# The first gated group's keys and values computed as blocks of Strassen's method beside the last cross-attention section

## The chip, the cores and the metric

The kernel runs on one core of one Trainium2 chip. The metric is the device time of one execution in microseconds (us). Five engines work side by side, each through its own queue in program order: PE (TensorE, matrix products), DVE (VectorE), ACT (ScalarE), POOL (GpSimd) and SP (SyncE, which here issues the transfers). They wait for each other through semaphores.

## The reference

Sixteen sequences of 128 tokens with 512 features, all in float32, pass through one decoder layer and one gated cross-attention layer:

```python
# decoder layer (16 heads of 32)
qkv = layernorm(x) @ w_qkv + b_qkv
x = x + attention(q, k, v, ltor_mask) @ w_ao + b_ao
q = layernorm(x) @ w_q + b_q;  k, v = split(ctx @ w_kv + b_kv)
x = x + attention(q, k, v, cross_mask) @ w_co + b_co
x = x + gelu(layernorm(x) @ w1 + b1) @ w2 + b2            # 512 -> 2048 -> 512
# gated layer
a = layernorm(ctx)
Q = x @ Wq.T;  K = a @ Wk.T;  V = a @ Wv.T
x = x + tanh(gate) * (attention(Q, K, V, key_mask) @ Wo.T)
```

## The kernel before

**Groups and sections.** The sixteen sequences are four groups of four (`NG`, `GB`). A section is one kind of attention for one group: A0 to A3 (self), B0 to B3 (cross), and, after the MLP, D0 to D3 (gated). `attend` runs the sections through one software pipeline. A section has 16 steps, 0 to 15, four for each sequence ("batch"); a unit is four heads of a batch, one per step. In `step` number k the following is put on the queues, in this order: at each fourth step the product of probabilities and values of an earlier batch (`av`, in `mix`) and the scores of a new one (`sc`, in `scores`); transfers that fetch turned probabilities (`receive_pair`); what was deferred by `afterwards` and is now run by `due()`; the jobs planned for this step; an output projection (`mo`); then the softmax of several units at once: `turn_unit` for unit k-3 (a DVE transpose and a transfer to DRAM, `away`), `norm_unit` for unit k-2 (a DVE reciprocal `sum`, then a POOL multiplication `s<-s,sum`), `least_unit` and `exp_unit` for unit k-1 (a DVE minimum `mn`, then four ACT exponentials), and `scale_unit` and `add_mask` for unit k (a DVE multiplication `s<-sc,mask`, then a POOL addition `s<-s,mask`). In the last batch of B3 the mask is instead added on DVE in four custom instructions with the minimum (`mask_and_least`), and POOL has no addition there.

**Jobs.** `jobs` of the next section, or `beside_last_cross` for B3, return a plan: which job is put on the queues in which step. The order on the queues is therefore written by hand, in lists of steps. `prepare` of a later object runs beside, one call per step: in B2's steps it is that of `FirstGated`, which normalizes the context of the first gated group (tile `T_a0`, four chunks scaled on ACT at steps 12 to 15) and fetches the turned weights `w_gk` and `w_gv`.

**Projections.** There are two ways to multiply weights with 512 tokens. `project_chunk` and `values_chunk` make one chunk of 128 outputs with four matmuls of 512 columns, and ACT copies the chunk out. `block_product` makes the same as seven products of half-size blocks (Strassen's method): four matmuls of 256 columns each, on sums of blocks that `left_blocks` and `right_blocks` describe as four additions on each side. Products 1, 6 and 7 collect in one PSUM bank and are copied out by ACT; products 5, 2, 4 and 3 are added by DVE to what stands there. The cross section's own keys and values are made in this way.

**Beside B3.** `gated_start` makes keys and values of the first gated group from `T_a0` (names `k_D0`, `v_D0`) by `project_chunk` and `values_chunk`, a chunk at each of steps 1, 2, 3, 5 and 7, 9, 13, 15, and keeps them in DRAM for later. `mlp_start` normalizes group 0 for the MLP (`ml_send`: DVE statistics, a POOL power `rstd_C`, a DVE `off_C`, an ACT scaling `ln_C`, a DVE transpose and a transfer) and gets it back turned (`back_C`, four ACT scalings to `T_C` at steps 12, 13, 14, 14). `piece` advances the generator `mlp`, which loads the first MLP weights, makes four sums of `w1_0` on POOL (`t<-w`), four sums of `T_C` on POOL (`sx`; `token_sums`), and from step 17 on the MLP's products `h`, in the order `H_ORDER`. The second of these reads the third `sx` sum. The MLP follows without a break.

Of the kernel before, what the change touches and what calls it, by code (L numbers as in the profile page):

```python
# [16 lines left out]
P = 128  # L17
# [37 lines left out]
def decoder_then_gated_cross_attention(ctx: ExitStack, tc: tile.TileContext, a: dict, out: bass.AP):  # L55
# [24 lines left out]
    def afterwards(engine, do):  # L80
        late[engine].append(do)
# [185 lines left out]
    def act_tile(name, tag="actT"):  # L267
        return work.tile([P, KC, TG], F32, tag=tag, name=f"T_{name}", bufs=2 if tag == "enc" else 1)
# [69 lines left out]
    def project_chunk(t, wt, actT, c, name, bias=None, bias0=0, bank="mm"):  # L338

        mm = ps(bank, f"mm_{name}_{c}")  # L340
        for k in range(KC):
            nc.tensor.matmul(mm, wt[:, k, c * P : (c + 1) * P], actT[:, k, :], start=(k == 0), stop=(k == KC - 1))
        if bias is None:
            afterwards("act", lambda: nc.scalar.copy(t[:, c], mm))
        else:
            afterwards("act", lambda: nc.scalar.activation(t[:, c, :], mm, AF.Identity, bias=col(bias, bias0 + c)))

    def values_chunk(v, wt, actT, b, name):

        mm = ps("mm", f"mm_{name}_{b}")  # L350
        for k in range(KC):
            nc.tensor.matmul(mm, actT[:, k, b * S : (b + 1) * S], wt[:, k, :], start=(k == 0), stop=(k == KC - 1))
        afterwards("act", lambda: nc.scalar.copy(v[:, b, :], mm))
# [17 lines left out]
    def left_blocks(wt, t):  # L371


        (a11, a21), (a12, a22) = halves(wt)
        s3, s2, s4, s1 = (*t, a21)[:4]
        return [a11, a12, s4, a22, s1, s2, s3], [
            (s3, a11, a21, ALU.subtract), (s1, a21, a22, ALU.add), (s2, s1, a11, ALU.subtract),
            (s4, a12, s2, ALU.subtract),
        ]
# [110 lines left out]
    def by_quarters(t):  # L490
# [18 lines left out]
        {10: (1,), 11: (2,), 12: (6,), 13: (5, 7), 15: (4, 3)},  # L509
    )  # L510
    FIRST_CROSS_BLOCKS = {6: (1,), 7: (2, 6), 8: (5,), 9: (7, 4), 11: (3,)}, CROSS_BLOCKS[1]
    GATED_BLOCKS = (
# [492 lines left out]
    class CrossAttention(Section):  # L1005
# [59 lines left out]

        v_bias = "b_cv", 0

        def tokens_again(self, at_, order=range(3)):
            return [([lambda b=b: fetch_part(f"x_{self.name}", x[self.g], b) for b in order], at_)]

# [74 lines left out]
    def mlp_start(ml):  # L1145

        ml.b2 = load_row(a["L0_xattn_b2"], "b2_row")
        ml.db1 = cpool.tile([P, NF], F32, tag="db1", name="db1")
        for i in range(NI):
            b1, c0 = columns["b1"]  # L1150
            c0 += i * KC
            nc.vector.tensor_tensor(
                ml.db1[:, 2 * i : 2 * i + 2], b1[:, c0 + 2 : c0 + 4], b1[:, c0 : c0 + 2], ALU.subtract
            )

        def row_difference():
            ml.db2 = work.tile([P, H], F32, tag="row", name="db2_row", bufs=2)
            nc.vector.tensor_tensor(ml.db2[:, 0:HF], ml.b2[:, HF:H], ml.b2[:, 0:HF], ALU.subtract)

        ml.lnT = []  # L1160
        def start():
            ml.lnT.append(act_tile("C0"))
            ml_begin(0)

        sends = [lambda b=b: ml_send(0, b) for b in range(GB)]
        back = [lambda k=k: chunk_back(ml.lnT[0][:, k], ml.back, k, "ln3_s", "ln3_b") for k in range(KC)]
        return (
            ([start, row_difference, lambda: ml_receive(0)], [0, 5, 7]), (sends, [0, 1, 2, 3]), (back, [12, 13, 14, 14]),
            ([lambda m=m: ml.part(m) for m in range(NQ)], [7, 7, 9, 9])
        )  # L1170

    def ml_begin(g):
# [2 lines left out]
    def ml_receive(g):  # L1175
        ml.back, ml.part = receiver(f"C{g}", ml.away)
# [4 lines left out]
    def mlp(ml, last_steps):  # L1181
# [8 lines left out]
        def sums_of(g, t):  # L1190
            s3, s2, s4 = (quarter(work, "s", f"sx{n}_{g}", 7) for n in range(3))
            quarters = [[t[i][:, :, j * HF : (j + 1) * HF] for j in range(2)] for i in range(2)]
            return token_sums(quarters, s3, s2, s4)
# [5 lines left out]
        def load(n, which):  # L1199
            g, i = steps[n]  # L1200
            ap, r0, c0 = (a["L0_xattn_w1"], 0, i * H) if which == 1 else (a["L0_xattn_w2"], i * H, 0)
            wt = wpool.tile([P, KC, H], F32, tag="w", name=f"w{which}_{n}")
            src = ap[r0 : r0 + H, c0 : c0 + H].rearrange("(k p) n -> p k n", p=P)
            if n < 2 and not (n == 1 and which == 2):
                for k in range(KC):
                    pieces.append(lambda k=k: nc.sync.dma_start(out=wt[:, k], in_=src[:, k]))
            elif g == 0:
                nc.sync.dma_start(out=wt, in_=src)
            else:
                nc.sync.dma_start(out=wt[:, 0:2, 0:HF], in_=src[:, 0:2, 0:HF])  # L1210
                nc.sync.dma_start(out=wt[:, 2:4, :], in_=src[:, 2:4, :])
            return wt
# [114 lines left out]

        w1[0] = load(0, 1)
        yield
        w2[0], w1[1] = load(0, 2), load(1, 1)  # L1330
        right1[0], todo, _ = sums(0, 1, "enc", w1.pop(0), nc.gpsimd)
        yield
        for do in todo:
            do()
            yield
        sides, todo = sums_of(0, [ml.lnT[0][:, 0:2], ml.lnT[0][:, 2:4]])
        for do in todo:
            do()
# [67 lines left out]
    def keep_part(key, t, n):  # L1406

        if n == 0:
            gated[key] = dram.tile(list(t.shape), F32, tag=f"kept_{key}", name=f"kept_{key}")
        nc.sync.dma_start(out=gated[key][:, n], in_=t[:, n])  # L1410
# [50 lines left out]
    class FirstGated:  # L1461


        def prepare(self, p):
            if p == 0:
                self.raw = work.tile([P, GB, H], F32, tag="enc", name="enc_D0", bufs=2)
                self.ln, self.away = ln_tile("D0"), away_tile("D0")
            if p in (0, 1):
                for b in (2 * p, 2 * p + 1):
                    nc.sync.dma_start(out=self.raw[:, b, :], in_=a["ctx_2048"][b])  # L1470
            elif p >= 2 * GB:
                key, k = ("gk", "gv")[p // GB - 2], p % GB
                if k == 0:
                    w[key] = wpool.tile([P, KC, H], F32, tag="w", name=f"w_{key}")
                nc.sync.dma_start(out=w[key][:, k], in_=gated[key][:, k])
            if 2 <= p < 6:
                q = p - 2
                normalize_and_send(self.raw[:, q, :], self.ln[:, q], self.away, "D0", q)
            if p >= 12:
                if p == 12:  # L1480
                    next(in_mlp)
                ml.pieces.popleft()()
            if p in (9, 11):
                if p == 9:
                    self.back, self.part = receiver("a0", self.away)
                for m in range(2):
                    self.part(m + 2 * (p == 11))
            if p >= 12:
                if p == 12:
                    self.aT = act_tile("a0", "enc")  # L1490
                group_back(self.aT, self.back, "gamma", "beta", [p - 12])

    def gated_start(first):

        first_k = work.tile([P, KC, TG], F32, tag="kT", name="k_D0", bufs=2)
        first_v = work.tile([P, GB, H], F32, tag="v", name="v_D0", bufs=2)

        def key_job(c):
            project_chunk(first_k, w["gk"], first.aT, c, "k_D0")
            afterwards("act", lambda: keep_later("k_D0", first_k, c, c != 1))  # L1500

        def value_job(b):
            values_chunk(first_v, w["gv"], first.aT, b, "v_D0")
            afterwards("act", lambda: keep_later("v_D0", first_v, b, True))

        def keep_later(key, t, n, wait):
            if wait:
                afterwards("act", lambda: keep_part(key, t, n))
            else:
                keep_part(key, t, n)  # L1510

        return (
            ([lambda c=c: key_job(c) for c in range(KC)], [1, 2, 3, 5]),
            ([lambda b=b: value_job(b) for b in range(GB)], [7, 9, 13, 15]),
        )

    class GatedAttention(Section):
# [206 lines left out]
    def beside_last_cross():  # L1724
        flip[0], in_blocks[0] = 2, False
        def piece():
            due()
            next(in_mlp)

        at_ = [2, 3, 4, 5, 6, 15, 15, 16, 16, 17, 18, 19, 19, 20, 21, 21, 22, 23, 23]  # L1730
        loads = [5, 7, 9, 11, 13, 14, 15, 16]
        return plan(
            *gated_start(first), *mlp_start(ml), *decoder[-1].tokens_again([1, 1, 3], (1, 0, 2)), ([piece] * len(at_), at_),
            ([lambda: ml.pieces.popleft()()] * len(loads), loads),
        )

# [94 lines left out]
```

## Time and profile before

| | us |
|---|---|
| median of 3 runs | 1154.2 |
| lowest and highest run | 1152.12, 1158.6 |
| profiled execution | 1150.03 |
| its span in the profile | 1148.3 |
| PE busy | 1127.4 (98%) |
| DVE, ACT, POOL busy | 743.3, 611.3, 695.4 |

The span runs from the first to the last instruction; 1.73 us of the profiled execution lie around it. PE is busy nearly all the time, so what counts is the short gaps in its row and the amount of its work. The granted clock of PE is at its full value in all slices. Times inside the span, such as 465.73, are microseconds from its start.

### The profile page before, as it was taken

What the parts mean: (1) busy time and instruction counts of PE and PEld (TensorE: products, weight loads), DVE (VectorE), ACT (ScalarE), POOL (GpSimd) and SP (SyncE); (2) the same over time, 40 slices, a digit from 0 to 9 for tenths busy, and PEclk for the clock granted to TensorE, in tenths of its full rate; (3) what the DMA queues carried; (4) which work ended last, traced back from release to release, by engine and by line L of the source; (5) the groups of instructions that cost most, each with busy time, mean ns of one, the idle gap of its engine ahead of it and who ended that gap; (6) DMA issues with size and microseconds to landing.
All of it is one profiled execution on the core that took longest, in us unless ns stands there. A gap on an engine that the chain in (4) does not pass through costs nothing. (4 is left out here: it accounts for less than half of the span.)

```text
span 1148.3 us, 22191 instructions
## 1 busy us (share of the span) xinstructions
PE 1127.4 (98%) x7246; PEld 870.1 (76%) x7246; DVE 743.3 (65%) x1919; ACT 611.3 (53%) x2142; POOL 695.4 (61%) x633
## 2 busy tenths in 40 slices
PE   8999999999999999999999999999999999999998
PEld 7877777667575757546788888888888877878885
DVE  6678988888877776987664634443342237767764
ACT  3467676767676776774231333233222337777663
POOL 6798888788868685773333414443343168545874
PEclk9999999999999999999999999999999999999999
DMA  6588878999888879999786596697446827988975
GB/s 222 153 216 233 221 217 221 260 231 264 211 229 217 229 213 255 294 284 296 243 259 232 183 285 188 198 280 266 156 147 220 268 70 191 246 245 233 266 223 182
DMA packets 325284, 259.81 MB, mean 226 GB/s; under 512 B 83560, under 2 KB 280624, under 8 KB 320304
## 3 DMA queue, kind: packets, MB, share of 16 engines
q1 hardware_dynamic: 325128, 258.38, 78.4%
q8 instruction: 58, 0.95, 0.4%
q14 instruction: 58, 0.48, 0.1%
q10 hardware_dynamic: 40, 0.01, 0.0%
HBM read 163.94 MB, written 94.37 MB: 225 GB/s over the span
## 5 line engine op out<-in xcount | busy, mean ns | idle before, releaser
L51 DVE TENSOR_TENSOR h<-h,h 128x512 f32<-128x512 f32 x80 | 54.8, 686 | 114.4 <-PE h L51 114.3
L51 ACT ACTIVATE h<-h 128x512 f32<-128x512 f32 x64 | 40.3, 630 | 160.9 <-DVE h L51 160.9
L51 ACT ACTIVATE s_A<-s_A,mn_A 128x128 f32<-128x128 f32 x256 | 99.4, 391 | 46.8 <-issue 24.1
L51 ACT ACTIVATE s_B<-s_B,mn_B 128x128 f32<-128x128 f32 x256 | 99.4, 392 | 31.1 <-issue 18.2
L51 POOL TENSOR_TENSOR s_D<-s_D,sum_D 128x512 f32<-128x512 f32 x64 | 66.8, 1043 | 56.1 <-DVE sum_D L51 53.7
L51 ACT ACTIVATE s_D<-s_D,mn_D 128x128 f32<-128x128 f32 x256 | 99.1, 392 | 0.4 <-issue 0.4
L51 POOL TENSOR_TENSOR s_B<-s_B,sum_B 128x512 f32<-128x512 f32 x64 | 67.2, 1051 | 51.5 <-DVE sum_B L51 33.5
L51 POOL TENSOR_TENSOR s_A<-s_A,sum_A 128x512 f32<-128x512 f32 x64 | 66.9, 1046 | 30.4 <-DVE sum_A L51 24.5
L51 POOL TENSOR_TENSOR s_A<-s_A,ma 128x512 f32<-128x512 f32 x64 | 82.3, 1286 | 5.1 <-DVE s_A L51 4.1
L51 POOL TENSOR_TENSOR s_B<-s_B,mask 128x512 f32<-128x512 f32 x60 | 76.8, 1280 | 2.2 <-DVE s_B L51 1.3
L51 POOL TENSOR_TENSOR rstd_aD<-rstd_aD,mhalf 128x1 f32<-128x1 f32 x12 | 6.6, 550 | 115.0 <-DVE rstd_aD L51 101.5
L51 POOL TENSOR_TENSOR sh<-h 128x512 f32<-128x512 f32 x32 | 40.8, 1274 | 50.5 <-ACT h L51 49.6
L51 PE MATMUL h<-T_C,w 128*128 128x256 f32 x256 | 61.2, 382 | 2.2 <-DVE h L51 2.2
L51 PE MATMUL h<-T_C,t 128*128 128x256 f32 x256 | 60.6, 379 | 1.0 <-DVE h L51 1.0
L51 PE MATMUL h<-sx,t 128*128 128x256 f32 x256 | 60.7, 380 | 0.5 <-POOL sx L51 0.5
L51 PE MATMUL o<-t,sh 128*128 128x256 f32 x256 | 60.5, 379 | 0.0
L51 PE MATMUL o<-w,h 128*128 128x256 f32 x256 | 60.5, 379 | 0.0
L51 PE MATMUL o<-t,h 128*128 128x256 f32 x256 | 60.5, 379 | 0.0
L51 DVE CUSTOM_DVE_ANT_0 s_D<-sc_D,gmask 128x128 f32<-128x128 f32 x256 | 57.2, 283 | 1.3 <-DMA turned_x<-x_D 0.7
L51 PE MATMUL mo_B<-w_co,mT_B 128*128 128x512 f32 x128 | 57.5, 592 | 0.0
L51 PE MATMUL mo_A<-w_ao,mT_A 128*128 128x512 f32 x128 | 57.5, 592 | 0.0
L51 PE MATMUL mm_q_B<-T_B,w_cq 128*128 128x512 f32 x128 | 57.4, 596 | 0.0
(335 smaller groups left out, 2998.1 us busy)
## 6 DMA issues: line engine op xcount, KB each, us to landing
t<-kept SPq DMA_DIRECT2D x24, 1024.0 KB, 8.2
away_A<-s_A SPq DMA_DIRECT2D x64, 256.0 KB, 3.1
pT_A<-away_A SPq DMA_DIRECT2D x128, 128.0 KB, 3.3
away_B<-s_B SPq DMA_DIRECT2D x64, 256.0 KB, 4.1
pT_B<-away_B SPq DMA_DIRECT2D x128, 128.0 KB, 3.3
away_D<-s_D SPq DMA_DIRECT2D x60, 256.0 KB, 3.6
pT_D<-away_D SPq DMA_DIRECT2D x120, 128.0 KB, 2.8
w<-in_L_xattn_w_dram SPq DMA_DIRECT2D x24, 512.0 KB, 5.9
```

The lines of the kernel that those rows point to most:

```text
L51: return lambda *args, **kw: self.tc.keep_in_program_order(call(*args, **kw))
```

## The change

Keys and values of the first gated group are now made by two block products, fourteen products in all, at the steps of a new table. Their sums are twelve additions on POOL: four of the tokens at steps 0, 0, 1, 2 (into three of group 3's batches `x3`, whose contents are kept in DRAM at this time), four of `w_gk` (three in B2's steps 13 to 15, by `FirstGated.prepare`, one in B3's step 3), and four of `w_gv` at steps 4 to 7. The four POOL sums of `w1_0` go from steps 3 to 6 to steps 8 to 11. The four normalizations for the MLP go from steps 0 to 3 to steps 1, 2, 4, 5, their return from 7, 7, 9, 9 to 9, 9, 10, 10, and a small row difference from step 5 to 7. The three batches of `x3` come back at steps 10, 11, 13 instead of 1, 1, 3. Finished keys are kept at steps 7 and 8, finished values at steps 16 and 17, where before each chunk was kept soon after it was made. PSUM banks for `av` and `mo` beside B3 are now the two of the tag `pt` alone.

```diff
+    FIRST_GATED_BLOCKS = (
+        {0: (1,), 1: (2, 6), 2: (5,), 3: (7, 4), 5: (3,)}, {9: (1, 5), 10: (6,), 11: (2,), 13: (7, 4), 15: (3,)},
+    )
...
+        def tokens_at(self):
+            return [x[self.g][:, b].rearrange("p (o t) -> p o t", t=HF) for b in range(3)]
...
-            ([start, row_difference, lambda: ml_receive(0)], [0, 5, 7]), (sends, [0, 1, 2, 3]), (back, [12, 13, 14, 14]),
-            ([lambda m=m: ml.part(m) for m in range(NQ)], [7, 7, 9, 9])
+            ([start, row_difference, lambda: ml_receive(0)], [0, 7, 9]), (sends, [1, 2, 4, 5]), (back, [12, 13, 14, 14]),
+            ([lambda m=m: ml.part(m) for m in range(NQ)], [9, 9, 10, 10])
...
-        w2[0], w1[1] = load(0, 2), load(1, 1)
+        w2[0] = load(0, 2)
         right1[0], todo, _ = sums(0, 1, "enc", w1.pop(0), nc.gpsimd)
         yield
         for do in todo:
             do()
             yield
+        w1[1] = load(1, 1)
+        yield
...
             if p >= 12:
                 if p == 12:
+                    self.key_sides, self.key_sums = left_blocks(w["gk"], decoder[NG].sums_at[0:3])
+                else:
+                    nc.gpsimd.tensor_tensor(*self.key_sums.pop(0))
...
-        def key_job(c):
-            project_chunk(first_k, w["gk"], first.aT, c, "k_D0")
-            afterwards("act", lambda: keep_later("k_D0", first_k, c, c != 1))
-
-        def value_job(b):
-            values_chunk(first_v, w["gv"], first.aT, b, "v_D0")
-            afterwards("act", lambda: keep_later("v_D0", first_v, b, True))
...
+        in_blocks[0] = True
+        right, todo = right_blocks(first.aT, decoder[-1].tokens_at())
+        key = block_product(halves(first_k), first.key_sides, right, False, "k_D0")
+        mask = work.tile([P, 2, 2, HF], F32, tag="mask", name="sums_gv", bufs=2)
+        left, sums = left_blocks(w["gv"], [mask[:, 0], mask[:, 1], sums_c])
+        value = block_product(by_quarters(first_v), left, right, True, "v_D0")
+        by_pool = lambda sums: [lambda o=o: nc.gpsimd.tensor_tensor(*o) for o in sums]
         return (
-            ([lambda c=c: key_job(c) for c in range(KC)], [1, 2, 3, 5]),
-            ([lambda b=b: value_job(b) for b in range(GB)], [7, 9, 13, 15]),
+            (by_pool(todo), [0, 0, 1, 2]), (by_pool(first.key_sums), [3]), (by_pool(sums), [4, 5, 6, 7]), *blocks_plan((key, value), FIRST_GATED_BLOCKS),
+            ([lambda n=n: keep_part("k_D0", first_k, n) for n in range(KC)], [7, 7, 8, 8]),
+            ([lambda n=n: keep_part("v_D0", first_v, n) for n in range(KC)], [16, 16, 17, 17]),
         )
...
-        at_ = [2, 3, 4, 5, 6, 15, 15, 16, 16, 17, 18, 19, 19, 20, 21, 21, 22, 23, 23]
+        at_ = [2, 8, 9, 10, 11, 11, 15, 15, 16, 16, 17, 18, 19, 19, 20, 21, 21, 22, 23, 23]
...
-            *gated_start(first), *mlp_start(ml), *decoder[-1].tokens_again([1, 1, 3], (1, 0, 2)), ([piece] * len(at_), at_),
+            *gated_start(first), *mlp_start(ml), *decoder[-1].tokens_again([10, 11, 13]), ([piece] * len(at_), at_),
```

More of the change, by code (lines that the diff above doesn't have):

```diff
@@ L1489, in prepare @@
                 if p == 12:
+                    self.key_sides, self.key_sums = left_blocks(w["gk"], decoder[NG].sums_at[0:3])
+                else:
+                    nc.gpsimd.tensor_tensor(*self.key_sums.pop(0))
+                if p == 12:
                     self.aT = act_tile("a0", "enc")
@@ L1496, in gated_start @@
         first_v = work.tile([P, GB, H], F32, tag="v", name="v_D0", bufs=2)
-        def key_job(c):
-            project_chunk(first_k, w["gk"], first.aT, c, "k_D0")
-            afterwards("act", lambda: keep_later("k_D0", first_k, c, c != 1))
-        def value_job(b):
-            values_chunk(first_v, w["gv"], first.aT, b, "v_D0")
-            afterwards("act", lambda: keep_later("v_D0", first_v, b, True))
[L1506 to L1510, printed above, removed]
+        in_blocks[0] = True
[5 more added lines that the diff above has]
+        by_pool = lambda sums: [lambda o=o: nc.gpsimd.tensor_tensor(*o) for o in sums]
         return (
-            ([lambda c=c: key_job(c) for c in range(KC)], [1, 2, 3, 5]),
-            ([lambda b=b: value_job(b) for b in range(GB)], [7, 9, 13, 15]),
+            (by_pool(todo), [0, 0, 1, 2]), (by_pool(first.key_sums), [3]), (by_pool(sums), [4, 5, 6, 7]), *blocks_plan((key, value), FIRST_GATED_BLOCKS),
+            ([lambda n=n: keep_part("k_D0", first_k, n) for n in range(KC)], [7, 7, 8, 8]),
+            ([lambda n=n: keep_part("v_D0", first_v, n) for n in range(KC)], [16, 16, 17, 17]),
         )
```

## The prediction

> **What bounds the kernel now.** I read the page's table of busy time first, then the timeline of PE around the changed stage, then POOL's and DVE's. PE is busy 98% of the span, so the first question is how much PE work goes away; the second is where PE already waits.
>
> ```profile
> 494.39 1.17 PE L51 MATMUL sc_B<-k_B,q_B 32*128 32x128 f32 x32
> 495.49 3.70 PE L51 MATMUL mm_v_D<-w_gv,T_a 128*128 128x512 f32 x8
> 499.03 3.60 PE L51 MATMUL mo_B<-w_co,mT_B 128*128 128x512 f32 x8
> 504.46 1.07 PE L51 MATMUL av_B<-pT_B,v_B 128*32 128x128 f32 x28 [1.49 <-DMA pT_B<-away_B]
> 523.96 1.99 PE L51 MATMUL h<-sx,t 128*128 128x256 f32 x8 [0.47 <-POOL sx L51]
> 527.35 1.07 PE L51 MATMUL av_B<-pT_B,v_B 128*32 128x128 f32 x28 [1.06 <-DMA pT_B<-away_B]
> ```
>
> Start, duration, operation, and in brackets the idle time before it with its releaser. One chunk (4 matmuls, shown as 8) takes about 3.5 us. Beside B3, PE already waits for the softmax at 504.46, and at 523.96 for the third POOL sum `sx`. So the softmax chain is as late as PE here: what makes that chain later is paid in full, and what PE saves before 523.96 is worth nothing unless the chain gets earlier too. After 565 PE has no gap for hundreds of us, so a delay at 524 reaches the end.
>
> ```profile
> 464.07 1.04 POOL L51 TENSOR_TENSOR s_B<-s_B,sum_B 128x512 f32<-128x512 f32 x1 [0.26 <-DVE sum_B L51]
> 468.71 0.55 POOL L51 TENSOR_TENSOR rstd_C<-rstd_C,mhalf 128x1 f32<-128x1 f32 x1 [2.37 <-DVE rstd_C L51]
> ...
> 488.39 1.28 POOL L51 TENSOR_TENSOR t<-w 128x512 f32<-128x512 f32 x1
> 489.63 1.05 POOL L51 TENSOR_TENSOR s_B<-s_B,sum_B 128x512 f32<-128x512 f32 x1
> 490.63 1.27 POOL L51 TENSOR_TENSOR s_B<-s_B,mask 128x512 f32<-128x512 f32 x1
> 491.85 1.28 POOL L51 TENSOR_TENSOR t<-t,w 128x512 f32<-128x512 f32 x1
> ...
> 498.16 1.04 POOL L51 TENSOR_TENSOR s_B<-s_B,sum_B 128x512 f32<-128x512 f32 x1 [0.58 <-DVE sum_B L51]
> 501.19 1.04 POOL L51 TENSOR_TENSOR s_B<-s_B,sum_B 128x512 f32<-128x512 f32 x1 [0.65 <-DVE sum_B L51]
> 507.37 1.27 POOL L51 TENSOR_TENSOR s_B<-s_B,mask 128x512 f32<-128x512 f32 x1
> 522.64 1.27 POOL L51 TENSOR_TENSOR sx<-T_C 128x512 f32<-128x512 f32 x1
> ```
>
> Steps 3 to 6, with one `t<-w` sum each, run on POOL without a gap: from 488.39 to 491.85 a step takes 3.46 us = sum 1.24 + norm 1.00 + mask 1.22. Steps without a sum (498.16 to 501.19, then to 503.71) take 2.5 to 3.0, set by the round trip DVE minimum, ACT exponentials, DVE reciprocal. A sum in a step therefore costs the softmax some 0.7 us a step.
>
> ```profile
> 465.70:481.70 16.00, 16.00 (x100) 7.79 (x96) 15.02 (x38) 9.88 (x38) 10.07 (x12) 1.00 0.96 279
> 481.70:494.40 12.70, 12.70 (x99) 6.29 (x91) 10.55 (x20) 9.27 (x39) 12.70 (x12) 1.00 0.99 286
> 494.40:505.40 11.00, 9.51 (x84) 4.90 (x80) 8.49 (x18) 7.84 (x35) 9.49 (x9) 1.00 1.04 268
> 505.40:518.00 12.60, 12.60 (x91) 6.27 (x88) 11.14 (x42) 11.67 (x46) 6.63 (x7) 1.00 1.09 304
> ```
>
> These are B3's four batches: length, then busy time of PE, weight load, DVE, ACT, POOL; at the end clock, DMA share, GB/s. The first is DVE's (15.02 of 16.00), the second POOL's, the third the softmax round trip's, the fourth PE's with DVE and ACT close behind.
>
> **PE's work.** Removed: 8 chunks; two of them ran from 466.83 to 473.80, so 3.49 each, 27.9 us. Added: 14 products; those of B3's own keys follow each other at 1.73 us (438.18, 439.91, 441.63, 443.36), 24.2 us. PE saves 3.7 us. It leaves batch 2 (steps 4 to 7) with one product and 5.2 us less work, just where POOL is full.
>
> **POOL's work.** Added: 12 sums at 1.24 us, 14.9 us. The first key sum lies in a POOL gap of 3.91 us before 458.50 and costs nothing. From the mask at 459.60 to the end of the last mask addition at 508.64, 49.0 us pass. In them POOL has 15 masks x 1.235 + 14 norms x 1.00 + 4 sums x 1.235 + 4 powers x 0.51 (480.77 to 481.28) = 39.5 us; 9.5 us are gaps. The eleven other sums add 13.6 us, 4.1 us more than the gaps hold. POOL takes its queue in order and the moved sums of `w1_0` are still ahead of step 12, so the last mask addition ends at least 4.1 us later, if nothing makes POOL wait at all. It will wait somewhat: a normalization needs DVE's statistics, then POOL's power, then DVE's offset, and at step 2 that power stands behind a 1.24 us token sum while DVE waits with its next reciprocal behind it. Going through steps 1 and 2 by these rows, I get about one such wait of 1.3 us left; the later steps have full POOL queues. So +4.1 to +5.4; I take +5.0, near the walk.
>
> The moves of the four normalizations (about 2.4 us of DVE each) are in this: they take one from step 0 and one from step 3 and so relieve the first batch, where DVE is the limit, but the time won there is filled by POOL's sums. The `x3` transfers, 256 KB each, go from steps 1 and 3 to 10 to 13 and SP then waits for PE's products 5, 6 and 4; PE has run these by then (it is ahead of the softmax), so the probability transfers queued behind on SP lose nothing; if PE were behind, up to a product, 1.7 us. The second half of `back_C` is issued at step 10 in place of 9 and has to land before ACT's scaling at step 12 (median 5.5 us to landing against two steps of 3.5): it fits by 1 to 2 us; if it fails, ACT's exponentials behind it are late by as much.
>
> **DVE's work.** ACT loses two copies of 0.57 us. DVE gets eight additions, one operand in PSUM, 0.60 us by their distance (466.35 to 466.95), 4.8 us. The four for keys fall into steps 2 to 6 under POOL's full queue and cost 0. Those of values fall into steps 11 to 15. One comes before the last minimum, in POOL's shadow. Three come after it:
>
> ```profile
> 508.67 0.69 DVE L51 TENSOR_REDUCE mn_B<-s_B 128x4 f32<-128x512 f32 x1
> 509.27 0.68 DVE L51 TENSOR_TENSOR s_B<-sc_B,mask 128x512 f32<-128x512 f32 x1
> ```
>
> From this minimum, which starts as the last mask addition ends (508.64), to the reciprocal at 521.43 that releases the norm ahead of `sx`, DVE is busy with one gap of 0.27 us. So three additions put 1.8 us on the path; 1.5 if that gap takes its part. The custom instructions of step 14 wait for POOL in this stretch both before and after.
>
> **A rule weighed.** The small row difference reads two SBUF operands and took 1.28 us for 128x256 while POOL was summing. The Trainium skill, "SBUF — State Buffer", in its summary of rules, says that a DVE instruction with two SBUF inputs blocks for the whole of a GpSimd instruction that reads SBUF; it speaks against filling POOL. By this rule the five differences for the MLP's biases could each wait out one sum. That would be 6.2 us instead of their 3.3 us in the trace, and the total 2.9 us higher if it all lay on the path. I keep the trace's figure. Without the rule: four differences took 1.98 us beside two POOL instructions at 464.44, so five beside a full POOL are bounded by no change and five POOL instructions, 5 x 1.24 = 6.2, less the 3.3 us they take now; most stays hidden under POOL's queue, and I take 0.
>
> **The sum.** At the `h` product of 523.96: +5.0 (POOL) +1.8 (DVE) = +6.8 us. The chain of probabilities (527.35) moves alike. PE's 3.7 us turn into waiting: between steps 4 and 12 PE stands still until DVE has read a bank of `pt` or the probabilities land. Three gaps follow between 541 and 565 (0.78, 1.45 and 0.98 us, all for DVE's additions to `h`); the first is a bank's turnover and stays, of the other 2.4 a fifth may go as loads then come earlier relative to PE: -0.5. Total +6.3 us: 1150.03 + 6.3 = 1156.3 for an execution like the profiled one, which is 4.2 below the median of the runs; set on the median, 1154.2 + 6.3 = 1160.5 us.
>
> **The rivals.** *PE decides (0.10).* The softmax keeps up and PE cashes its saving: -3.7, with the gaps of 1.49 and 1.06 perhaps shrinking, to -6.2: 1148.0 to 1150.5, not slower. For it: PE is 98% busy and the fourth batch is PE's. Against it: 13.6 us of sums in 9.5 us of gaps. It decides if the sums take less than 0.86 us each (9.5/11) beside other work; the trace has none under 1.24. *Late but absorbed (0.12).* POOL ends 4.1 late, the DVE additions cost 1.5, and the contention of step 14 (four instructions took 3.4 instead of 0.9 us, 2.5 lost) mostly goes because POOL meets other instructions; with part of the two later gaps: 4.1 + 1.5 - 2.0 - 1.5 = +2.1: 1156.3. *Returns too late (0.16).* `back_C` or `x3` land after ACT or DVE need them, with transfers already at a share of 1.04 to 1.10; one median landing of 5.5 us less the slack of 1.5 is +4.0 more: +10.3, 1164.5. *POOL decides (0.62)*: +3.5 to +9, my forecast.
>
> **How the numbers follow.** A difference of 0.5%, 5.8 us, is about what a measurement of this kernel can tell from none. Of the forecast's 0.62 about two thirds lie above it (0.40), with all of the late returns (0.16): slower 0.56. Faster by more needs the far end of the first rival: 0.05. The rest, 0.39, is within. The range leaves out most of the first rival at the bottom and the end of the last at the top: 1152.5 (POOL absorbed, and the runs' own scatter of 2 us) to 1167.5 (late returns, with the biases' waits of 2.9).
>
> **What would show it.** In the profile after: POOL without gaps from 464 to some 512, its last mask addition in B3 ending at 512.7 to 514 instead of 508.64; steps 4 to 11 of 3.5 us throughout; PE gaps of several us before the `av` or `mo` of steps 6 to 12, together above 6 us between 466 and 524; the `h<-sx` product at 529 to 531 with a wait for POOL `sx`; PE after 565 as before. My prediction is wrong if PE has no more idle time beside B3 than its 2 us now, or if POOL's sums start behind gaps, or if that product starts before 526.

## The result, and the profile after

| | before | after |
|---|---|---|
| median of 7 runs each (us) | 1154.2 | 1161.94 |
| lowest and highest run | 1150.44, 1158.6 | 1160.65, 1165.26 |
| ratio after to before, 95% interval | | 1.0080 [1.0065, 1.0094] |
| profiled execution (us) | 1150.03 | 1164.54 |
| its span | 1148.3 | 1162.8 |
| start of the first `h<-sx` product | 523.96 | 534.57 |
| end of the last mask addition of B3 | 508.64 | 517.27 |

The kernel became 0.8% slower, 7.7 us by the medians; 1160.5 was forecast. The two profiled executions are 14.5 us apart because before's is near the low end of its runs and after's near the high end of its own. So places inside the two spans are compared below, and the size of an effect is taken from medians.

The timeline of PE in the kernel after, beside B3 (start, duration, operation, idle time before it with its releaser):

```profile
471.10 2.58 PE L51 MATMUL mm_k_D<-T_a,w_gk 128*128 128x256 f32 x8 [2.25 <-DVE v_B L51]
493.70 1.07 PE L51 MATMUL av_B<-pT_B,v_B 128*32 128x128 f32 x28 [0.80 <-DMA pT_B<-away_B]
496.69 2.04 PE L51 MATMUL sc_B<-k_B,q_B 32*128 32x128 f32 x26 [1.50 <-DVE s_B L51]
498.66 3.78 PE L51 MATMUL mm_v_D<-w_gv,T_a 128*128 128x256 f32 x8
506.32 1.97 PE L51 MATMUL mm_v_D<-sums_gv,x 128*128 128x256 f32 x8 [1.80 <-ACT v_D L51]
511.56 1.89 PE L51 MATMUL mm_v_D<-w_gv,T_a 128*128 128x256 f32 x8
524.92 1.97 PE L51 MATMUL mm_v_D<-sums_c,T_a 128*128 128x256 f32 x8 [2.28 <-DVE v_D L51]
534.57 1.99 PE L51 MATMUL h<-sx,t 128*128 128x256 f32 x8 [1.31 <-POOL sx L51]
```

PE, which before had 1.49 and 0.47 us of idle time on this way, now waits six times for 0.8 to 2.3 us up to `h<-sx`, whose own wait is for POOL. Only one of the others is for probabilities. The rest are for banks and results that DVE and ACT still hold: product 6 of the values (506.32) for ACT's copy of product 1, product 3 (524.92) for a DVE addition. One product (498.66) took 3.78 instead of 1.9 us.

POOL's timeline shows all its idle time above 0.2 us from 459.81 to the last mask addition, which is the last row:

```profile
459.81 1.04 POOL L51 TENSOR_TENSOR s_B<-s_B,sum_B 128x512 f32<-128x512 f32 x1 [4.77 <-DMA pT_B<-away_B]
472.31 1.04 POOL L51 TENSOR_TENSOR s_B<-s_B,sum_B 128x512 f32<-128x512 f32 x1 [0.62 <-DVE sum_B L51]
481.55 1.04 POOL L51 TENSOR_TENSOR s_B<-s_B,sum_B 128x512 f32<-128x512 f32 x1 [1.10 <-ACT ln_C L51]
500.93 1.04 POOL L51 TENSOR_TENSOR s_B<-s_B,sum_B 128x512 f32<-128x512 f32 x1 [1.04 <-DVE sum_B L51]
515.99 1.28 POOL L51 TENSOR_TENSOR s_B<-s_B,mask 128x512 f32<-128x512 f32 x1
```

And three rows of DVE's timeline:

```profile
466.31 4.05 DVE L51 TENSOR_TENSOR db<-vcols 128x2 f32<-128x2 f32 x4
497.66 2.52 DVE L51 TENSOR_TENSOR db_row<-b_row 128x256 f32<-128x256 f32 x1
513.49 0.69 DVE L51 TENSOR_TENSOR v_D<-mm_v_D,v_D 128x512 f32<-128x512 f32 x1 [1.04 <-PE mm_v_D L51]
```

The four small differences for the MLP took 4.05 us (1.98 before), the row difference 2.52 (1.28 before). The addition at 513.49 waits for product 2, which PE ran only at 511.56, and the transpose and reciprocal of step 12 stand behind it on DVE.

Three stretches of the kernel after by windows, cut by time and no longer by batch (length; busy time of PE, weight load, DVE, ACT, POOL; then clock, DMA share, GB/s):

```profile
465.70:481.70 16.00, 13.75 (x77) 10.00 (x75) 14.66 (x29) 8.48 (x33) 14.07 (x14) 0.89 0.65 173
481.70:494.40 12.70, 11.90 (x126) 8.28 (x126) 12.21 (x29) 8.78 (x38) 12.70 (x13) 1.00 0.77 213
494.40:511.00 16.60, 13.30 (x75) 9.62 (x66) 13.26 (x24) 9.33 (x40) 15.56 (x14) 0.79 0.97 277
```

POOL is now full or nearly so in all three (14.07 of 16.00, 12.70 of 12.70, 15.56 of 16.60), and PE's granted clock, 1.00 in before's four batches, falls to 0.89 and 0.79 in two of them.

### The profile page after: what moved, and what is told of

It reads as the page before. It is cut to its first block, busy times and chain, and to the rows that moved or that the text cites. A ratio compares the mean times of both kernels' runs of the same rounds, so it can differ in the third digit from the quotient of the medians.

```text
span 1162.8 us, 22302 instructions
## 1 busy us (share of the span) xinstructions
PE 1131.4 (97%) x7294; PEld 883.6 (76%) x7294; DVE 751.3 (65%) x1927; ACT 610.2 (52%) x2140; POOL 708.9 (61%) x645
## 4 chain that ended last, share of the span: by engine, by line
PE 43%; POOL 4%; issue 4%; DMA 3%; DVE 2%; ACT 1%; SPq 1%; POOLq 0%; DVEq 0%
PE o L51 16%; PE h L51 15%; PE mm_v_D L51 3%; PE mm_q_D L51 3%; POOL x L51 1%; PE mm_k_D L51 1%; DMA away_D<-s_D 1%; POOL s_D L51 1%; PE av_D L51 1%; PE mo_D L51 1%; PE sc_D L51 1%; SPq L51 1%; PE mm_o_D L51 1%; DMA pT_D<-away_D 1%; DVE s_D L51 1%
```

## The experiments

The theory at the start was that of the prediction: POOL's additional sums make the softmax chain late, and PE's saving is worth nothing. The rivals: the two-input differences that wait for POOL (the port), PE's clock, and, from the rows above, a ring in which PE, ACT and DVE wait for each other through the in-place additions of the values' products. Twelve kernels were run. All medians and intervals stand in one table, with two places of each profiled execution; `h<-sx` is the start of the first such product, the mask column the end of the last mask addition of B3.

| run | median us | ratio to before, 95% | mask | `h<-sx` | PE clock |
|---|---|---|---|---|---|
| before (profile) | 1154.2 | | 508.64 | 523.96 | 1.000 |
| after (profile) | 1161.94 | 1.0080 [1.0065, 1.0094] | 517.27 | 534.57 | 0.994 |
| e1, differences elsewhere | 1162.17 | 1.0078 [1.0060, 1.0096] | 515.26 | 532.74 | 0.994 |
| e2, without the `w1_0` sums | 1164.46 | 1.0100 [1.0083, 1.0116] | 517.01 | 534.31 | 0.994 |
| e3, the same in before | 1151.18 | 0.9992 [0.9979, 1.0004] | 506.96 | 524.25 | 1.000 |
| e4, four products twice | 1166.72 | 1.0127 [1.0105, 1.0148] | 518.33 | 535.63 | 1.000 |
| e5, moves alone | 1152.92 | 1.0000 [0.9987, 1.0013] | 507.93 | 524.43 | 0.999 |
| e6, keys alone | 1162.39 | 1.0074 [1.0058, 1.0091] | 514.30 | 529.90 | 0.996 |
| e7, values' products earlier | 1162.88 | 1.0082 [1.0067, 1.0096] | 518.01 | 534.79 | 0.997 |
| e8, before with less PE work | 1153.68 | 0.9999 [0.9988, 1.0010] | 508.94 | 524.84 | 0.999 |
| e9, without the twelve sums | 1156.36 | 1.0028 [1.0015, 1.0040] | 511.12 | 528.51 | 0.996 |
| e10, without the keys' eight sums | 1160.92 | 1.0061 [1.0039, 1.0083] | 513.22 | 530.67 | 0.997 |
| e11, e7 and e2 together | 1160.22 | 1.0061 [1.0040, 1.0083] | 515.08 | 530.97 | 0.998 |
| e12, e7 and e9 together | 1157.18 | 1.0036 [1.0022, 1.0050] | 511.28 | 528.82 | 0.996 |

From `h<-sx` to the end of the span, executions of kernels of both kinds scatter between 624 and 630 us, so the column tells by itself only differences of several us. Sizes below go by the ratio, 0.1% being 1.15 us; by it the change cost 9.2 us, by the medians of the first seven runs 7.7.

**e1: the port.** The four differences go to a step of section A0, the row difference to step 20.

```diff
-            nc.vector.tensor_tensor(ml.db1[:, 2 * i : 2 * i + 2], ...)   # when the vectors are ready, beside B3
+    def bias_differences(): ...                                          # the same four, in step 11 of A0
-            ([start, row_difference, lambda: ml_receive(0)], [0, 7, 9]),
+            ([start, row_difference, lambda: ml_receive(0)], [0, 20, 9]),
```

> The changed kernel, with the five bias differences taken out of B3's first steps: the four of db1 made on DVE in A0's step 11, the row difference in B3's step 20. Theory POOL queue (eleven sums too many in POOL's gaps, then three DVE additions): POOL's queue is full either way, so 0 to -1 us against the changed kernel, some 1161 to 1162. Theory port (the differences have two SBUF inputs and wait out POOL's sums: in the changed profile 4.05 us in place of 1.98 for the four and 2.52 in place of 1.28 for the row, and the softmax queue stands behind them on DVE): -2.5 to -3.5 us, some 1158.5 to 1159.5, and the wait of PE for DVE before product 2 of the keys (2.25 us) gone. Theory clock (PE's granted clock falls to 0.89 and 0.79 in the two stretches with PE gaps, and slow products cost the time): 0 to -1 us.

The rows of 4.05 and 2.52 us are gone, and so are POOL's gaps of 0.62 and 1.04 us. The last mask addition ends 2.0 us earlier, `h<-sx` starts 1.8 earlier, without a wait for POOL. The time did not change: 1.0078 against 1.0080. The waits of 2.28 us for DVE (522.92) and 1.04 us of DVE for product 2 are still there, and that product 3 took 3.62 us instead of 1.97. The wait for POOL is real, but its 2 us do not reach the end measurably; the two intervals are wide enough to hide some 2 us.

**e2 and e3: less work on POOL in steps 8 to 11.** The four sums of `w1_0` are left out of both kernels.

```diff
+                if n == 0 and which == 1:
+                    (b11, b12), (b21, b22) = halves(wt)
...
+                    return [b11, b21, b22, b12, b12, b12, b12], [lambda: None] * 4, None
```

> The changed kernel without the four POOL sums of w1_0 at steps 8 to 11 (group 0 uses unsummed blocks in their place: this part of the computation is left out). Theory POOL queue: the last mask addition of B3 comes 4 x 1.24 = 5.0 us earlier if POOL's queue decides alone; the steps can't get shorter than the round trip of 2.7 us against 3.5 now, so 3 to 4 us of it: -3 to -4 us against the changed kernel, some 1158 to 1159. Theory port: 0 to -1. Theory clock: 0 to -1.

> The kernel before without the four POOL sums of w1_0 at steps 3 to 6 (the same part is left out). Theory POOL queue: steps 3 to 6 take 2.8 in place of 3.5 us on POOL, 2.8 us in all, but PE is nearly full there, so 0 to -2 us against before: 1152.2 to 1154.2. If POOL were as binding before as after, -3 to -4.

In the kernel after nothing is won (1.0100; if anything lost), though POOL has 4.9 us less to do. The timelines of its POOL and DVE tell why:

```profile
509.44 1.26 POOL L51 TENSOR_TENSOR s_B<-s_B,mask 128x512 f32<-128x512 f32 x1
514.74 1.04 POOL L51 TENSOR_TENSOR s_B<-s_B,sum_B 128x512 f32<-128x512 f32 x1 [4.04 <-DVE sum_B L51]
```

```profile
511.50 0.69 DVE L51 TENSOR_TENSOR x<-x,mo_B 128x512 f32<-128x512 f32 x1 [1.88 <-PE mo_B L51]
513.23 0.69 DVE L51 TENSOR_TENSOR v_D<-mm_v_D,v_D 128x512 f32<-128x512 f32 x1 [1.04 <-PE mm_v_D L51]
```

The mask of step 11 is added by 510.70, as early as hoped. But the next normalization waits 4.04 us for DVE's reciprocal, which stands behind two additions that wait for PE: the output projection, late because product 6 ahead of it waited for ACT, and product 2. A second chain of the same length lay under POOL's queue. In before the sums cost nothing measurable either (0.9992), so POOL alone was not its bound.

**e4: more work on PE.** Two products of the keys and two of the values are issued twice, 6.9 us.

```diff
-            for o in range(2):
+            for _ in range(2 if (name, n) in (("k_D0", 5), ("k_D0", 4), ("v_D0", 5), ("v_D0", 2)) else 1):
+              for o in range(2):
```

> The changed kernel with PE running four of the fourteen products twice (keys 5 and 4, values 5 and 2; the repetition starts its bank anew, so the outcome is the same): 4 x 1.73 = 6.9 us more work on PE, more than the 3.7 us that the method saves. Theory POOL queue: PE's gaps beside B3 (some 11 us) take it: 0 to +1 us against the changed kernel, some 1162 to 1163. Theory clock: PE keeps its clock with fewer gaps: -1 to -3 us. If PE's amount of work decides: +5 to +7 us.

The time rises by 0.47 points of a per cent, 5.4 us of the 6.9; the ends of the two intervals allow 1 to 10 us. The profiled executions do not show where: the last mask addition and `h<-sx` come only 1.1 us later than in the kernel after (518.33, 535.63). There the clock is at 1.000 with PE's gaps filled, and products that took 2.58, 3.00 and 3.78 us in the kernel after take 1.97, 1.89 and 1.99. Up to `h<-sx`, then, most of the added work took the place of waits and slow products, and a full clock with this work did not bring these places forward. What the other 4 us are is not shown.

**e5: the moves alone.** The kernel before, with chunks for keys and values, but normalizations, returns, row difference and `w1_0` sums in the steps of the change.

```diff
-            ([start, row_difference, lambda: ml_receive(0)], [0, 5, 7]), (sends, [0, 1, 2, 3]), ...
-            ([lambda m=m: ml.part(m) for m in range(NQ)], [7, 7, 9, 9])
+            ([start, row_difference, lambda: ml_receive(0)], [0, 7, 9]), (sends, [1, 2, 4, 5]), ...
+            ([lambda m=m: ml.part(m) for m in range(NQ)], [9, 9, 10, 10])
-        at_ = [2, 3, 4, 5, 6, 15, 15, 16, 16, 17, 18, 19, 19, 20, 21, 21, 22, 23, 23]
+        at_ = [2, 8, 9, 10, 11, 15, 15, 16, 16, 17, 18, 19, 19, 20, 21, 21, 22, 23, 23]
```

> The kernel before with the change's moves alone: the four normalizations for the MLP in steps 1, 2, 4, 5, their return in 9, 9, 10, 10, the row difference in step 7, the four sums of w1_0 in steps 8 to 11. Keys and values stay chunks. If the ring between PE and DVE that the values' products make (product 2 in front of step 12's reciprocal, product 3 behind DVE's masks) costs the time, the moves cost nothing: -1 to +1 us against before. If the moved sums and normalizations on POOL and DVE cost it, whatever the products do: +2 to +4 us, with a last mask addition after 510 instead of 508.64.

Nothing: 1.0000 [0.9987, 1.0013]. The cost is with Strassen's products, their sums, and what comes with them: `av`, `mo` and the products share the two banks of `pt`, `x3` comes back later, and keys and values are kept later. None of these three was run alone.

**e6: keys alone.** Values by four chunks, on the banks `mm0` and `mm1`, without the `w_gv` sums.

```diff
-            ... (by_pool(sums), [4, 5, 6, 7]), *blocks_plan((key, value), FIRST_GATED_BLOCKS),
+            ... ([lambda b=b: values_chunk(first_v, w["gv"], first.aT, b, "v_D0", ("mm0", "mm1")[b % 2]) for b in range(GB)], [7, 9, 13, 15]),
+            *blocks_plan((key,), FIRST_GATED_BLOCKS[:1]),
```

> The kernel after with Strassen's method for the keys alone; values by four chunks in steps 7, 9, 13, 15 as before, without the four POOL sums of w_gv (these values then read tokens that the key sums have already overwritten by a quarter, so only the time is read). POOL has 8 sums more than before instead of 12, DVE 4 additions instead of 8, PE 1.9 us less than before instead of 3.7. If the cost is made by the values' products (ring of PE and DVE in steps 9 to 15): most of it goes, +1 to +3 us against before, no wait of 2.28 us, h<-sx at 525 to 528. If the first half makes it (key sums, bias differences, late steps 0 to 5): +5 to +8 us, h<-sx at 530 or later.

The keys alone cost as much as the whole change, 1.0074. The ring of the values is thus not needed for the loss. Here the chain of probabilities is what PE waits for, twice (PE's timeline):

```profile
508.80 1.07 PE L51 MATMUL av_B<-pT_B,v_B 128*32 128x128 f32 x28 [3.58 <-DMA pT_B<-away_B]
511.48 4.75 PE L51 MATMUL mm_v_D<-w_gv,T_a 128*128 128x512 f32 x8
...
534.17 1.92 PE L51 MATMUL av_B<-pT_B,v_B 128*32 128x128 f32 x28 [2.04 <-DMA pT_B<-away_B]
```

A wait of 3.58 us, a chunk of 4.75 instead of 3.7 us behind it, and after `h<-sx` again 2.04 us of waiting and slow operations.

**e7: the ring taken apart.** The same products, the values' at earlier steps.

```diff
-        ... {9: (1, 5), 10: (6,), 11: (2,), 13: (7, 4), 15: (3,)},
+        ... {6: (1,), 7: (5,), 8: (2,), 9: (6,), 11: (7, 4), 13: (3,)},
```

> The kernel after with the values' products at earlier steps: 1 at 6, 5 at 7, 2 at 8, 6 at 9, 7 and 4 at 11, 3 at 13, in place of 1, 5 at 9, 6 at 10, 2 at 11, 7, 4 at 13, 3 at 15. The same work on every engine. If the ring of PE and DVE is the cost: the waits of 2.28 (product 3 for DVE), 1.80 (product 6 for ACT) and 1.04 us (DVE for product 2) go or shrink, h<-sx comes 2 to 4 us earlier than in the kernel after, and the time is +4 to +6 us against before. If the softmax is late for another reason (POOL's amount, the port, the first batch), PE only waits elsewhere: +7 to +9 us.

PE's waits for DVE and ACT at products 3 and 6 are gone, and the time is the same, 1.0082: PE waits elsewhere, 2.00 us for ACT before an output projection (504.59) and 3.50 us for probabilities (525.74). POOL's queue now holds the softmax to the end: without a gap above 0.6 us from 501.30, its last mask addition ends at 518.01. One of the additions still waits on DVE, for ACT's copy of product 7 (1.04 us). After the wait of 3.50 us three operations took 1.92, 3.78 and 3.79 us, where before has 1.07, 1.99 and 3.60; so part of what the ring had cost came back as slow operations.

**e8: less work on PE, in the kernel before.** Three of four matmuls of the last key chunk and of the first value chunk are left out, 5.2 us.

```diff
-        for k in range(KC):
+        K = 1 if (name, c) == ("k_D0", 3) else KC
+        for k in range(K):
...
+        K = 1 if (name, b) == ("v_D0", 0) else KC
```

> The kernel before with 5.2 us of PE's work beside the third batch of B3 and the second left out: three of four matmuls of the last key chunk (step 5) and of the first value chunk (step 7); those keys and values are then partial sums. If PE's saving is worth nothing because the softmax chain is as late (the prediction's reading): 0 to -1 us. If PE is the bound beside B3: -3.5 to -5 us.

The time is the same, 0.9999 [0.9988, 1.0010]. PE waits instead, among others 3.04 us for probabilities before the `av` at 505.96, where the kernel before waited 1.49.

**e9 and e10: without POOL's sums.** e9 leaves out all twelve sums, e10 the eight for the keys.

```diff
+    def raw_left(wt):
+        (a11, a21), (a12, a22) = halves(wt)
+        return [a11, a12, a12, a22, a21, a21, a21]
...
-                    self.key_sides, self.key_sums = left_blocks(w["gk"], decoder[NG].sums_at[0:3])
+                    self.key_sides, self.key_sums = raw_left(w["gk"]), []
...
-        right, todo = right_blocks(first.aT, decoder[-1].tokens_at())
+        right, todo = raw_right(first.aT), []
-        left, sums = left_blocks(w["gv"], [mask[:, 0], mask[:, 1], sums_c])        # e9 only
+        left = raw_left(w["gv"])                                                  # e9 only
...
```

> The kernel after with the twelve POOL sums for the first gated group's keys and values left out (the products read plain blocks, so these keys and values are other numbers). Products, copies and DVE additions stay where they are. If POOL's amount of work is the cause: the last mask addition ends at 509 to 511 as in before, h<-sx starts at 524 to 527, time 0 to +3 us against before. If the products' places on PE and DVE, or the clock, are the cause: +5 to +9 us, with the wait of 2.28 us for DVE still there.

> The kernel after with only the eight sums for the keys left out (four of w_gk, four of the tokens; both keys and values are then other numbers); the four sums of w_gv stay in steps 4 to 7. Eight sums are 9.9 us, of which one lies in a free gap. If POOL's amount is the cause, what is left (4 sums, 5.0 us, in 9.5 us of gaps) is nearly absorbed: +1 to +4 us. If the values' half costs: +6 to +9 us.

Without any of the sums the ratio falls from 1.0080 to 1.0028 [1.0015, 1.0040]: the sums cost 0.52%, 6 us (by the ends of the two intervals 3 to 9), and 3.2 us are left. In e9 PE's timeline shows what is left:

```profile
498.52 3.63 PE L51 MATMUL mm_v_D<-w_gv,T_a 128*128 128x256 f32 x8 [2.66 <-ACT v_D L51]
505.41 1.89 PE L51 MATMUL mm_v_D<-w_gv,T_a 128*128 128x256 f32 x8
518.69 3.59 PE L51 MATMUL mm_v_D<-w_gv,T_a 128*128 128x256 f32 x8 [2.19 <-DVE v_D L51]
```

The ring again: product 6 waits 2.66 us for ACT and then runs at half speed, product 2 (505.41) is late for DVE, which waits 1.04 us for it, product 3 waits 2.19 us.

A second wait lies behind `h<-sx`. These are the `av` of B3's last batch in PE's timelines of before, after, e9 and e12, in this order:

```profile
545.12 1.40 PE L51 MATMUL av_B<-pT_B,v_B 128*32 128x128 f32 x32
557.16 1.07 PE L51 MATMUL av_B<-pT_B,v_B 128*32 128x128 f32 x28 [1.47 <-DMA pT_B<-away_B]
551.54 1.07 PE L51 MATMUL av_B<-pT_B,v_B 128*32 128x128 f32 x28 [1.99 <-DMA pT_B<-away_B]
551.42 1.07 PE L51 MATMUL av_B<-pT_B,v_B 128*32 128x128 f32 x28 [2.58 <-DMA pT_B<-away_B]
```

All ten profiled kernels that have products of the change wait here, 0.84 to 2.98 us; the four with chunks for all keys and values of the gated group (before, e3, e5, e8) wait 0 to 0.30. Between 541 and 580 PE's gaps add up to 3.4 to 5.5 us in the ten and to 1.8 to 3.2 in the four. In the kernel after, SP issues four transfers that keep `v_D` at 534.58 and 536.66, shortly before these last probabilities; in before the last two of them are issued at 516.93. No run moves them, so the cause of this wait is not shown.

With the four `w_gv` sums kept (e10) most of the loss is back, 1.0061. Keys alone cost 8.5 us (e6), and the values' sums add 3.8 to what e9 has left (0 to 8 by the intervals). So the parts do not add up to the whole. PE's timeline of e10 shows a wait that is not a matter of POOL's amount of work alone:

```profile
500.59 3.51 PE L51 MATMUL mm_v_D<-sums_gv,T_a 128*128 128x256 f32 x8 [4.87 <-ACT v_D L51]
```

Product 6 waits 4.87 us for ACT's copy, which stands behind exponentials (from 495.78), these behind a minimum (495.05), and this on DVE behind the row difference, which took 2.53 us (491.91). In e9, without sums beside it, the row difference took 0.41 us and product 6 waited 2.66. How much of e10's loss this wait makes was not tested.

**e11 and e12: both chains opened.** e11 is e7 without the `w1_0` sums of e2, e12 is e7 without the twelve sums of e9; their edits are those shown.

> The kernel with the values' products at earlier steps, and without the four POOL sums of w1_0 (the MLP's first products then read plain blocks). Taking these sums out alone, or moving the products alone, gained nothing. If each only uncovered the other (POOL's queue and the ring of PE and DVE end within 2 us of each other): now -3 to -5 us against the kernel after, +4 to +6 against before. If neither matters: +7 to +9 us.

> Both at once: the values' products at the earlier steps 6, 7, 8, 9, 11, 13, and the twelve POOL sums for keys and values left out (the products read plain blocks). If POOL's sums and the ring of PE, ACT and DVE are together the whole cost: last mask addition ends at 508.5 to 510.5, h<-sx starts at 524 to 526.5, time -1 to +1.5 us against before. If something else of the change (additions on DVE, PE's clock, later transfers) costs what was left without the sums: +2 to +4 us, with h<-sx at 527 or later.

e11: what e2 or e7 alone did not move at all moves now, `h<-sx` by 3.6 us (534.57 to 530.97); the median is 1160.22, at 1.0061, but its interval overlaps that of the kernel after, so the time leans to the theory and does not prove it. The profiled execution is also the fastest of e11's six.

e12 comes out on the second branch of its expectation, at its upper end: 1.0036, +4.2 us, `h<-sx` at 528.82, no better than e9. So POOL's sums and the ring at products 2, 3 and 6 are together not the whole cost. PE's timeline and the window of these rows:

```profile
519.62 1.92 PE L51 MATMUL av_B<-pT_B,v_B 128*32 128x128 f32 x28 [4.11 <-DMA pT_B<-away_B]
521.47 3.78 PE L51 MATMUL h<-T_C,w 128*128 128x256 f32 x8
525.05 3.94 PE L51 MATMUL mo_B<-w_co,mT_B 128*128 128x512 f32 x8
528.82 1.89 PE L51 MATMUL h<-sx,t 128*128 128x256 f32 x8
```

```profile
519.50:530.00 10.50, 10.38 (x50) 7.08 (x51) 8.62 (x16) 5.02 (x24) 8.79 (x7) 0.70 0.92 264
```

Moving the products away left PE with little work in the last batch (8.35 us busy in the 13.80 before this window). After a wait of 4.11 us it ran at a granted clock of 0.70: three operations took 1.92, 3.78 and 3.94 us that elsewhere take 1.07, 1.99 and 3.60, 3.0 us more, and `h<-sx` started late with no wait for POOL. In this execution the ring was exchanged for a slow clock; it is the slowest of e12's five, 3.2 us above their median, so the others may not show it in this size. No run holds the clock fixed, so how the 3 to 4 us that remain in e9 and e12 divide between DVE's additions, the waits of PE, that of the last `av` among them, and the clock stays open.

## Why the prediction was right, and which of its terms were not

**The forecast** was 1160.5, slower; measured 1161.94, and the whole interval of the ratio lies above 1.005. The path was right in the main: the softmax chain decides, POOL's sums make it late, and PE's saving is worth nothing. That the size came so near (+7.7 by the medians, +6.3 forecast) is partly luck. In the profiled pair the `h` product moved by 10.6 us, not 6.8, and waits of PE for ACT and DVE that the sum does not have are in the measured time, as are later stalls that grew.

**"What PE saves before 523.96 is worth nothing."** Shown by e8: 5.2 us taken out bring 0.0. The other direction is not settled: in the kernel after 6.9 us more cost 5.4 by the ratio, but moved `h<-sx` by only 1.1 in the profiled execution (e4).

**POOL +5.0.** The size agrees: without the sums 6 us go (e9, 3 to 9 by the intervals). Its working was only half right. From the mask at 460.92 to the end of the last at 517.27, 56.3 us pass, against the 49.0 of before: +7.3. POOL's own work is the predicted 39.5 + 13.6 = 53.1 us; the remaining 3.2 are gaps, where the prediction left one of 1.3. Those of 0.62 and 1.04 us are the biases' waits, as e1 shows; the third, 1.10, is the normalization's.

**"The moved sums of `w1_0` are still ahead of step 12."** This step failed as a cause: e2 took them away and nothing came earlier. The prediction said that PE is ahead of the softmax when the `x3` transfers of steps 10 to 13 wait for its products. In fact the products' banks tie PE to ACT's copies and DVE's additions, and product 2 ran at 511.56, so that the additions, put on DVE's queue ahead of step 12's transpose and reciprocal, waited for PE. Two chains ended together; the prediction saw one.

**The count of gaps.** Filling 9.5 us of gaps with 13.6 us of sums would leave seven key sums (8.6 us) alone, or four value sums (5.0), free. They were not: +8.5 us (e6) and +7.0 us (e10), products included; e9's products without any sum cost 3.2. The gaps of before lie mostly in steps 0 to 3 and in the third batch, and that a sum costs in the step where it stands fits this, though no run moves one sum of the change to show it; the sum over the whole stretch came out right only for all of them together.

**DVE +1.8.** From the end of the last mask addition to the start of the third `sx` sum, 14.00 us before and 15.98 after (533.25): +1.98, the size that was given. Most of it by the trace is the additions' 0.6 us each. In e7, e11 and e12, which leave one addition in this stretch, it takes 14.57 us, and in e6, which has none, 13.60. (e5, with none, takes 15.18: there DVE waits 1.46 us for ACT's exponentials in this stretch.) But PE's `av` of the next batch also went back by product 3's 2.28 us of waiting for one of these additions, which the prediction did not have.

**Bias differences 0.** The durations doubled, 1.98 to 4.05 and 1.28 to 2.52, as the rule in the Trainium skill, "SBUF — State Buffer", summary of rules, would have it; by it they would take 6.2 us together; they took 6.57. The row difference after waited out two POOL instructions, one more than the rule gives it (last section). The 1.28 us of before did not lie beside a sum, as the prediction reads it, but beside a normalization and a mask. On POOL's queue these waits were 1.7 us of gaps. Taking them away changed the time by nothing measurable (e1), so 0 was right for the end, and wrong for the mechanism.

**Later stalls -0.5.** None went: PE's gaps between 541 and 575 are 0.78, 1.47, 1.28 and 0.85 us, one more than before and 1.2 us more in all. The new one is the last `av`'s wait for probabilities, which e9 and e12 have too.

**The lines that would show it.** POOL nearly without gaps to 513: seen. The last mask addition at 512.7 to 514: 517.27, missed. Of this 1.3 us are a later first normalization (459.81 against 458.50). Executions of e3, e5 and e8 show 0.3 to 0.9 of it (458.81 to 459.39); in the kernel after ACT waited longer for `back_a` there (until 457.11 against 455.79). Whether the change has a part in this is not shown. PE gaps above 6 us between 466 and 524: 7.7 us, but at products and scores, hardly at `av` and `mo`. `h<-sx` at 529 to 531 with a wait for `sx`: 534.57, later than that, with the wait. The rival of returns too late did not happen: ACT's scaling of `back_C` starts without a wait at 518.06.

None of the kernels tried beats the kernel before; the one with the moves alone equals it.

## What to carry to other kernels

Before saving work on the busiest engine, take some of that work out and see whether the time moves; here 5 us less on an engine that was 98% busy moved nothing. A saving that is paid with sums on an engine inside the critical loop is better counted step by step, at the places where the sums stand, than against the total of the gaps. And products that add in place onto others' results tie three queues together: when removing one bottleneck changes nothing, look for the first wait that now stands in its place, and remove both before judging either.

## What was not expected of the hardware

**A two-input DVE operation can wait out two POOL instructions in a row.** The row difference took 0.41 us where POOL had no sums (e9, 492.04), 2.52 after and 2.53 in e10. In the kernel after it started at 497.66 and ended at 500.18; POOL's mask (497.41) and sum (498.63) followed each other without a gap and ended at 499.89, so it did not get in between. In before it did. Its row and POOL's two rows beside it:

```profile
486.03 1.28 DVE L51 TENSOR_TENSOR db_row<-b_row 128x256 f32<-128x256 f32 x1
485.97 1.05 POOL L51 TENSOR_TENSOR s_B<-s_B,sum_B 128x512 f32<-128x512 f32 x1
486.97 1.47 POOL L51 TENSOR_TENSOR s_B<-s_B,mask 128x512 f32<-128x512 f32 x1
```

It ended at 487.31, 0.29 us after the normalization, and the mask behind took 1.47 us instead of 1.27. What decides between the two cases is not shown. The four bias differences took 1.97 us in e9 and 4.05 after, where POOL ran four instructions without a gap beside them (465.62 to 470.33): 0.61 to 1.30 us each, about one POOL instruction for each difference.

**PE's clock can fall after waits of some 2 us.** In the kernel before the mean clock of the span is 1.000. Behind waits of 2.25 us, 0.80 + 1.50 us (after), 2.66 and 2.19 us (e9) or 4.11 us (e12), operations took up to twice their time for some 3 to 9 us. The wait alone does not decide: after waits of 2.28 us (before 524.92 in after) and 3.04 us (before 505.96 in e8) the next operations ran at their usual speed. The Trainium skill, "TensorE: Matmul & The Clock Gate", in its part on the clock gate, has a clock that halves when PE is idle over a window of about 3.4 us; the halved speed agrees with these rows (3.63 against 1.89 us), the length of the waits, mostly shorter, does not.
